# A third Strassen step for one raw product of blocks, and PSUM cut into three pairs and two single banks

## The chip, the cores and the metric

The kernel runs on one core of one Trainium2 chip. The metric is device time in microseconds of one execution. TensorE (PE) multiplies, VectorE (DVE) and ScalarE (ACT) read its sums out of PSUM and prepare its operands, SyncE (SP) issues most of the transfers.

## The reference, cut to what matters

Input x has 8 sequences of 256 rows and 1024 columns, all in float32. Layer one adds a dense product, a routed adapter of rank 16 per expert (two of eight experts per row) and x itself; layer two adds a product with one of 16 dense weights, chosen for each sequence:

```python
# layer one
base = jnp.einsum('btd,od->bto', x, W)
logits = jnp.einsum('btd,ed->bte', x, Wr) + bias[:, None, :]
topw, topi = jax.lax.top_k(logits, 2)
weights = jax.nn.softmax(topw, axis=-1)
gates = jnp.sum(jax.nn.one_hot(topi, E) * weights[..., None], axis=-2)
h = jnp.einsum('btd,erd->bter', x, A)
x = x + base + 2.0 * jnp.einsum('bter,bte,eor->bto', h, gates, B)
# layer two
w = weight[adapter_ids]
x = x + jnp.einsum('bsi,boi->bso', x, w)
```

## The kernel before, in words

Nothing is left to a scheduler: the order of the Python calls is the order of each engine's queue (a manual schedule). The tile layer puts semaphores between the engines where tiles are shared.

**Layer one** is W (1024 x 1024) times x (1024 x 2048 tokens). It is cut into 2 x 2 blocks and done with Winograd's form of Strassen's scheme: seven products of blocks, called "1" to "7", in the order 1, 5, 2, 6, 3, 7, 4. Product 1 is `opening` (L398), the other six are calls of `product` (L442). Each product (512 x 512 by 512 x 1024) is again cut into 2 x 2 and done with seven smaller products, each of four 128x512 matmuls: two row groups m by two depths k. The sums of blocks that these need are s1 to s3 (of W's blocks) and t1 to t3 (of x's blocks), made on VectorE by `make_subs` (L336); `late` (L358) turns s2 and t2 into the fourth sums. In `product` the seven stand in this order, by PSUM tile: A = a00 x b00; B = s1 x t1; A += s2 x t2; X = a01 x b10; A += s3 x t3; B += s2 x b11 (s2 is the fourth sum by now); A += a11 x t2. So a00 x b00 and a01 x b10 (X) are the two products of raw blocks. After each, `evict` (L372) adds the PSUM tile into a quarter of the result y on VectorE (L183), or, where there is nothing to add to, copies it on ScalarE (L375).

A PSUM tile is `bank` (L87): 128 partitions x 2 x 512 float32, so two of the eight banks; the pool turns four of them round.

In four of the six (5, 2, 3, 4) two more matmuls per quarter add the adapter's rows, from `hg` (the gated inner values, turned) and `b_sb` or `bdiff` (L379 to 395).

**The adapter** is prepared between product 1 and product 5. `project(j, c)` (L203) multiplies a quarter of the tokens by the adapter and router weights, 32 matmuls of 136 columns into one PSUM tile; VectorE then makes the logits `lg`, and ScalarE copies the rest to `hT`. `gating(j)` (L249) is some twenty small VectorE instructions and one of 1024 columns. `turn(j)` (L282) turns hT with eight TensorE transposes and copies them to `hg` on ScalarE, in one instruction:

```python
def turn(j):
    ps_g = bank(f"ps_g_{j}")
    for n in range(C):
        nc.tensor.transpose(ps_g[:, n // CQ, ts(n % CQ, P)], hT[j][:, n, :], ident)
    nc.scalar.copy(hg[j], ps_g)
```

The calls between the products stand at L644 to L697: project(1, 0), project(1, 1), gating(1), the sums of product 5 on VectorE, project(0, 1), turn(1), product 5, turn(0), product 2.

**What VectorE does besides.** `todo` is a list of VectorE work for later products (sums of blocks of W and x, the sub-sums of the next product, joins of results). `pump(place)` (L305) stands after each of the seven smaller products and puts an even share of what is left into VectorE's queue there; each entry has a cost and a first place at which it may go.

**Layer two** (`adapt`, L531) does the same for each of the eight sequences with one Strassen step. It uses the same four PSUM tiles, but only half of each. The last sequence (`adapt_last`, L589) splits three of its products into 256-column halves (tile A_last).

Of the kernel before, what the change touches and what calls it, by code (L numbers as in the profile page):

```python
# [9 lines left out]
F32 = mybir.dt.float32  # L10
# [15 lines left out]
def kernel(  # L26
# [48 lines left out]
    sub2 = ctx.enter_context(tc.tile_pool(name="sub2", bufs=2))  # L75
    rpool = ctx.enter_context(tc.tile_pool(name="rpool", bufs=1))
    psum = ctx.enter_context(tc.tile_pool(name="psum", bufs=4, space=PSUM))

# [5 lines left out]
    def flat(blk):  # L84
        return blk.rearrange("p k n -> p (k n)")

    def bank(name):  # L87
        return psum.tile([P, 2, TQ], F32, name=name, tag="acc")

# [9 lines left out]
    aw_sb = flat(yb["12"])[:, : KC * EA].rearrange("p (k e) -> p k e", k=KC)  # L99
    hT = [flat(yb["11"])[:, j * C * ER : (j + 1) * C * ER].rearrange("p (c e) -> p c e", c=C) for j in range(2)]  # L100
    b_sb = const.tile([ER, O], F32, name="b_sb")
    ids = const.tile([1, 2, NB], I32, name="ids")
# [82 lines left out]
    def add(out_, x, y):  # L185
        tt(out_, x, y, ALU.add)

    def minus(out_, x, y):
        tt(out_, x, y, ALU.subtract)
# [7 lines left out]
    hg = [const.tile([ER, 2, TQ], F32, name=f"hg{j}") for j in range(2)]  # L197
    lg = [rpool.tile([P, C, E], F32, name=f"lg_{j}", tag=f"lg{j}") for j in range(2)]
    gate8 = {}

    projected = {}

    def project(j, c, *some, first=True, last=True):  # L203


        if first:
            projected[j, c] = bank(f"ps_h_{j}_{c}")
        ps = projected[j, c]
        some = some or range(KC)
        for k in some:  # L210
            for r in range(CQ):
                v, u = divmod(r, 2)
                nc.tensor.matmul(  # L213
                    ps[:, v, u * EA : (u + 1) * EA],
                    lhsT=xk(k, j, c)[:, ts(r, P)],
                    rhs=aw_sb[:, k, :],
                    start=(first and k == some[0] and u == 0),
                    stop=(last and k == some[-1]),
                    skip_group_check=True,
                )  # L220
        if not last:
            return
        ps = ps[:, :, : 2 * EA].rearrange("p v (u e) -> p v u e", u=2)
        split = lambda t: t[:, c * CQ : (c + 1) * CQ, :].rearrange("p (v u) e -> p v u e", v=2)
        nb = CQ * P // S
        b0 = (2 * j + c) * nb
        add(
            split(lg[j]),
            ps[:, :, :, ER:],
            bias[:, b0 : b0 + nb, :].unsqueeze(2).to_broadcast([P, nb, CQ // nb, E]),  # L230
        )
        nc.scalar.copy(split(hT[j]), ps[:, :, :, :ER])

    def first_max(src, j, n):

        m = rpool.tile([P, C], F32, name=f"m{n}_{j}", tag=f"m{n}")
        place = rpool.tile([P, C, E], F32, name=f"place{n}_{j}", tag=f"place{n}")
        first = rpool.tile([P, C], F32, name=f"first{n}_{j}", tag=f"first{n}")
        hot = rpool.tile([P, C, E], F32, name=f"hot{n}_{j}", tag=f"hot{n}")
        wide = [P, C, E]  # L240
# [8 lines left out]
    def gating(j):  # L249

        m1, hot1, ops1 = first_max(lg[j], j, 1)
        rest = rpool.tile([P, C, E], F32, name=f"rest_{j}", tag="rest")
        m2, hot2, ops2 = first_max(rest, j, 2)
        dm = rpool.tile([P, C], F32, name=f"dm_{j}", tag="dm")
        ex = rpool.tile([P, C], F32, name=f"ex_{j}", tag="ex")
        den = rpool.tile([P, C], F32, name=f"den_{j}", tag="den")
        g1 = rpool.tile([P, C], F32, name=f"g1_{j}", tag="g1")
        g2 = rpool.tile([P, C], F32, name=f"g2_{j}", tag="g2")
        wide = [P, C, E]
# [21 lines left out]

    def turn(j):  # L282

        ps_g = bank(f"ps_g_{j}")
        for n in range(C):
            nc.tensor.transpose(ps_g[:, n // CQ, ts(n % CQ, P)], hT[j][:, n, :], ident)  # L286
        nc.scalar.copy(hg[j], ps_g)

# [46 lines left out]

    def make_subs(key, w, x):  # L336

# [5 lines left out]
        def b(i, j):  # L343
            return xb[x][:, 2 * i : 2 * i + 2, j * TQ : (j + 1) * TQ]

        t = {}

        def op(name, fn, x, y, first):
# [8 lines left out]

        def late():  # L358
            minus(t["s2"], a(0, 1), t["s2"])
            minus(t["t2"], b(1, 0), t["t2"])  # L360

        subs[key] = (a, b, t, late)
        return [
            op("s1", add, a(1, 0), a(1, 1), 2),
            op("t1", minus, b(0, 1), b(0, 0), 2),
            op("s2", minus, "s1", a(0, 0), 2),
            op("t2", minus, b(1, 1), "t1", 2),
            op("s3", minus, a(0, 0), a(1, 0), 5),
            op("t3", minus, b(1, 1), b(0, 1), 5),
        ]  # L370

# [7 lines left out]
    def multiply(up=None, tokens=None):  # L379


        def mm(acc, lhs, rhs, first=False, rows=None, c=0, part=(0, 1)):
            steps = [(lhs[:, k, ts(m, P)], rhs[:, k, :], m) for k in part for m in range(2)]
            if up is not None and rows is not None:
                steps += [(up[rows][:, ts(m, P)], hg[tokens][:, c, :], m) for m in range(2)]
            for i, (l, r, m) in enumerate(steps):
                nc.tensor.matmul(  # L387
                    acc[:, m, :],
                    lhsT=l,
                    rhs=r,  # L390
                    start=(first and i < 2),
                    stop=(i >= len(steps) - 2),
                    skip_group_check=True,
                )

        return mm

    def opening(key, dest):  # L398


        idle = bank("idle")
        for i in range(WARM):
            nc.tensor.matmul(idle[:, 0, :P], lhsT=ident, rhs=ident, start=True, stop=True)  # L403
        mm = multiply()
        sums_of = make_subs(key, "11", "11")
        a, b, t, late = subs.pop(key)
        X = bank(f"X_{key}")
        A = bank(f"A_{key}")
        add_identity(wb["11"], 0, 2)
        mm(X, a(0, 1), b(1, 0), True, part=(0,))  # L410
        project(0, 0, 2, last=False)
        mm(X, a(0, 1), b(1, 0), part=(1,))
        evict(dest[:, 0], X)
        project(0, 0, 3, first=False, last=False)
        mm(A, a(0, 0), b(0, 0), True, part=(0,))
        project(0, 0, 0, first=False, last=False)
        mm(A, a(0, 0), b(0, 0), part=(1,))
        project(0, 0, 1, first=False, last=False)
        use_adapter_ids()
# [5 lines left out]
        use_ids(idle[:, 1, :NB])  # L425
        B = bank(f"B_{key}")
        mm(B, t["s1"], t["t1"], True)
# [4 lines left out]
        evict(dest[:, 1], A)  # L432
        project(0, 0, *range(KH, KC), first=False)
        late()
        mm(A, t["s3"], t["t3"])
# [6 lines left out]
    def product(key, base, dest, lora=None, tokens=None):  # L442

        a, b, t, late = subs.pop(key)
        mm = multiply(dict(zip("01d", b_part(lora))) if lora is not None else None, tokens)
        old = [base[:, q] if base is not None else None for q in range(4)]
        A = bank(f"A_{key}")
        mm(A, a(0, 0), b(0, 0), True)
        evict(dest[:, 0], A, old[0])
        pump(1)  # L450
        B = bank(f"B_{key}")
        mm(B, t["s1"], t["t1"], True, "1", 1)
        evict(dest[:, 3], B, old[3])
        pump(2)
        mm(A, t["s2"], t["t2"])
        evict(dest[:, 1], A, old[1])
        pump(3)
        X = bank(f"X_{key}")
        mm(X, a(0, 1), b(1, 0), True, "0", 0)
        add(dest[:, 0], X, dest[:, 0])  # L460
        late()
        pump(4)
# [68 lines left out]
    def adapt(u):  # L531
# [3 lines left out]
        w = rawset[u % 2]  # L535
        accs = {}

        def mm(name, lhs, rhs, first=False):
            if first:
                accs[name] = bank(f"{name}1_{u}")[:, 0, :]  # L540
            for k in range(KH):
# [47 lines left out]
    def adapt_last(half, sy, w, z, mm, store):  # L589
# [3 lines left out]
        m = OG // 2  # L593
        accs = [bank(f"A{v}_last")[:, 0, :m] for v in range(2)]
        c11, c12, c21, c22 = (z[i][:, ts(j, OG)] for i in range(2) for j in range(2))
# [53 lines left out]
    subs5[2][2]()  # L649
    project(1, 0)  # L650

# [3 lines left out]
    for k in range(KH):  # L655
        t1(0, k)
    project(1, 1)
    for t in gating(1):
# [4 lines left out]
    for k in range(2, KH):  # L663
        t1(1, k)
    subs5[3][2]()
    subs5[4][2]()
    subs5[5][2]()
    project(0, 1)
    turn(1)
    todo += gating(0)  # L670
    todo += w_sum(minus, "11", "21", "11")
    todo += make_subs("2", "12", "21")
    product("5", None, y22, 1, 1)
    turn(0)
    todo += x_sum(minus, "12", "22", "12")
# [10 lines left out]
    todo += make_subs("7", "21", "11")  # L686
    todo += x_sum(minus, "21", "21", "12")
    todo += join(y12, y21)
    product("3", y22, y12, 2, 1)
    load_w1(0, "12", "22", "11")  # L690
    todo += make_subs("4", "22", "21")
    todo += join(y22, y21)
# [62 lines left out]
```

## Time and profile before

| | us |
|---|---|
| median of 3 runs | 430.58 (430.48 to 431.51) |
| the profiled execution | 431.35 |
| its span | 429.6 |
| PE busy | 424.7 (1222 records; a float32 matmul is two) |
| DVE busy | 272.3 (331 instructions) |
| ACT busy | 32.6 (51 instructions) |
| layer one ends (chain) | 233.75 |

The chain of waits follows the work that ended last back from the end. An instruction on it moves the end when it gets longer. The timeline gives each instruction's start and length in microseconds from the start of the span, and in brackets how long its engine had been idle and who ended that.

### The profile page before, as it was taken

The page shows a single profiled execution, that of the slowest core. Times are in us where ns is not written, and L with a number is a line of the kernel's source. Part 1 is how long each engine was busy: PE and PEld are TensorE (multiplying, and loading weights), DVE is VectorE, ACT ScalarE, POOL GpSimd, SP SyncE. Part 2 cuts the span into 40 slices and gives each one's busy share as a digit, 9 for nine tenths or more (in the row PEclk, how much of TensorE's full clock was granted, in tenths as well). Part 3 has the DMA queues.
Part 4 walks back from the last instruction along what each step waited for, and adds up shares of the span by engine and source line. Part 5 has one row for each costly group of instructions (what it writes and reads, how often), then busy time and mean ns, then how long its engine had stood idle before and what let it go on. Part 6 is the DMA issues. An engine that isn't in the chain of part 4 may idle for free.

```text
span 429.6 us, 3225 instructions
## 1 busy us (share of the span) xinstructions
PE 424.7 (99%) x1222; PEld 212.7 (50%) x1222; DVE 272.3 (63%) x331; ACT 32.6 (8%) x51; POOL 2.0 (0%) x10
## 2 busy tenths in 40 slices
PE   8999999999999999999999999999999999999996
PEld 5566984444444444444444444444444444444574
DVE  2627395658877979779575676665756576665531
ACT  1110104010000000000000101010110101010110
POOL 1000000000000000000000000000000000000000
PEclk9999999999999999999999999999999999999999
DMA  8994000000000140630202276556748375550202
GB/s 287 381 400 206 2 2 0 0 0 0 2 0 0 35 160 2 243 148 0 98 2 98 98 256 224 206 201 204 278 140 309 140 268 220 195 198 0 98 0 98
DMA packets 14303, 55.81 MB, mean 130 GB/s; under 512 B 1232, under 2 KB 3536, under 8 KB 9808
## 3 DMA queue, kind: packets, MB, share of 16 engines
q1 hardware_dynamic: 12976, 54.68, 35.3%
q10 hardware_dynamic: 1248, 0.93, 0.7%
q8 instruction: 9, 0.15, 0.2%
q14 instruction: 6, 0.05, 0.0%
q0 software_dynamic: 64, 0.00, 0.0%
HBM read 47.22 MB, written 8.39 MB: 129 GB/s over the span
## 4 chain that ended last, share of the span: by engine, by line
PE 99%; POOL 0%; ACT 0%; issue 0%; POOLq 0%
PE A L387 24%; PE A L542 22%; PE B L387 14%; PE B L542 13%; PE X L387 8%; PE ps_h L213 7%; PE X L542 6%; PE A_last L600 3%; PE idle L403 1%; PE ps_g L286 0%; ACT z L630 0%; PE idle L424 0%; POOL ident masks.py:199 0%; POOL desc_i L149 0%; POOL ident masks.py:197 0%
## 5 line engine op out<-in xcount | busy, mean ns | idle before, releaser
L542 PE MATMUL B<-x,x 128*128 128x512 f32 x128 | 57.5, 592 | 0.0
L387 PE MATMUL A<-t,s 128*128 128x512 f32 x112 | 50.3, 592 | 0.0
L183 DVE TENSOR_TENSOR y<-A,y 128x1024 f32<-128x1024 f32 x23 | 28.1, 1223 | 20.1 <-PE A L387 20.1
L542 PE MATMUL A<-w,x 128*128 128x512 f32 x88 | 39.6, 592 | 0.0
L542 PE MATMUL A<-w,y 128*128 128x512 f32 x88 | 39.1, 592 | 0.0
L542 PEld LDWEIGHTS B<-x,x 128*128 128x128 f32 x128 | 24.3, 190 | 29.8 <-issue 29.7
L183 DVE TENSOR_TENSOR w<-w,w 128x1024 f32<-128x1024 f32 x24 | 29.0, 1222 | 15.4 <-PE A L542 15.3
L387 PEld LDWEIGHTS A<-t,s 128*128 128x128 f32 x112 | 21.2, 190 | 26.3 <-issue 26.3
L375 ACT COPY z<-A 128x512 f32<-128x512 f32 x21 | 12.3, 586 | 272.0 <-PE A L542 272.0
L213 PEld LDWEIGHTS ps_h<-y,x 128*128 128x128 f32 x256 | 30.7, 191 | 3.4 <-issue 3.4
L213 PE MATMUL ps_h<-y,x 128*128 128x136 f32 x256 | 30.6, 279 | 0.0
L542 PEld LDWEIGHTS A<-w,x 128*128 128x128 f32 x88 | 16.7, 190 | 21.0 <-issue 21.0
L542 PEld LDWEIGHTS A<-w,y 128*128 128x128 f32 x88 | 16.7, 190 | 21.0 <-issue 21.0
L387 PE MATMUL X<-x,w 128*128 128x512 f32 x56 | 27.1, 627 | 0.0
L387 PE MATMUL A<-x,w 128*128 128x512 f32 x56 | 25.3, 592 | 0.0
L387 PE MATMUL B<-t,s 128*128 128x512 f32 x56 | 25.3, 594 | 0.0
L387 PE MATMUL B<-x,s 128*128 128x512 f32 x56 | 25.2, 592 | 0.0
L387 PE MATMUL A<-t,w 128*128 128x512 f32 x56 | 25.2, 592 | 0.0
L183 DVE TENSOR_TENSOR y<-B,y 128x1024 f32<-128x1024 f32 x12 | 14.7, 1224 | 15.7 <-PE B L387 15.7
L183 DVE TENSOR_TENSOR x<-x,x 128x1024 f32<-128x1024 f32 (+1 forms) x20 | 19.3, 1004 | 0.0
L387 PEld LDWEIGHTS X<-x,w 128*128 128x128 f32 x56 | 11.0, 200 | 13.1 <-issue 12.8
L387 PEld LDWEIGHTS A<-t,w 128*128 128x128 f32 x56 | 10.6, 190 | 13.4 <-issue 13.4
(109 smaller groups left out, 398.3 us busy)
## 6 DMA issues: line engine op xcount, KB each, us to landing
x<-w_dram SPq DMA_DIRECT2D x24, 1024.0 KB, 4.8
w<-w_dram SPq DMA_DIRECT2D x8, 1024.0 KB, 4.7
out_dram<-z SPq DMA_DIRECT2D x15, 512.0 KB, 3.1
x<-xT_dram SPq DMA_DIRECT2D x6, 1024.0 KB, 13.6
w<-wT_dram SPq DMA_DIRECT2D x3, 1024.0 KB, 15.6
x<-xT_dram SPq DMA_DIRECT2D x4, 256.0 KB, 3.8
x<-xT_dram SPq DMA_DIRECT2D x2, 512.0 KB, 6.7
w<-w11T_dram SPq DMA_DIRECT2D x1, 512.0 KB, 5.4
```

The costliest lines, as they stand in the source:

```text
L183: nc.vector.tensor_tensor(out_, x, y, op)
L213: nc.tensor.matmul(ps[:, v, u * EA : (u + 1) * EA], lhsT=xk(k, j, c)[:, ts(r, P)], rhs=aw_sb[:, k, :], start=(first and k == some[0] and u ...
L375: nc.scalar.copy(dest, acc)
L387: nc.tensor.matmul(acc[:, m, :], lhsT=l, rhs=r, start=(first and i < 2), stop=(i >= len(steps) - 2), skip_group_check=True,)
L403: nc.tensor.matmul(idle[:, 0, :P], lhsT=ident, rhs=ident, start=True, stop=True)
L542: nc.tensor.matmul(accs[name], lhsT=lhs[:, k // 2, k % 2, :], rhs=rhs[:, k, :], start=(first and k == 0), stop=(k == KH - 1), skip_group_c ...
L600: nc.tensor.matmul(acc, lhsT=lhs[:, k // 2, k % 2, :], rhs=rhs[:, k, ts(v, m)], start=(first and k == 0), stop=(k == KH - 1), skip_group_c ...
```

## The change

Three things.

1. **X is computed by a third step.** In `product`, X = a01 x b10 (four 128x512 matmuls) becomes Winograd's seven products of 128 x 128 by 128 x 256. VectorE makes six sums per product for it beforehand (r1, r2, r4 with 128 columns, q1, q2, q4 with 256), and two more (r3, q3) inside it. ScalarE copies A (a00 x b00) into X's pair, and three of the seven are added onto that copy. The first product goes to a single bank, A3, the second and third of the scheme to B3 and A3 again. The first quarter of the result is put together from A3 (quarter by quarter), B3 and X on VectorE. B's matmuls are split: row group 0 before A's second product, row group 1 after it. `late` is split into its two sums, moved ahead of X.
2. **PSUM is laid out by name**: three pairs of banks (`pair0` to `pair2`) and two single banks. A, X and B change pairs from product to product (`roles`). The projections and turns take pairs or singles; their readers work half by half.
3. **The small tiles of the gating** move into a free part of y12, to make room for the deep sums; four sums of x21 are put into `todo` in two halves ("P5" in the list of the change is the split of B's product).

```diff
+    def pair(name, n):
+        return psum.tile([P, 2, TQ], F32, name=name, tag=f"pair{n}")
+    def single(name, n):
+        return psum.tile([P, TQ], F32, name=name, tag=f"single{n}")
+    def halves(pair_):
+        return [pair_[:, v, :] for v in range(2)]
+    def singles(name):
+        return [single(f"{name}{v}", v) for v in range(2)]
+    role = [2, 1, 0]
+    def roles(name):
+        a, x, b = role
+        role[:] = [x, b, a]
+        return lambda which: pair(f"{which}_{name}", dict(A=a, X=x, B=b)[which])
...
-        add(
-            split(lg[j]),
-            ps[:, :, :, ER:],
-            bias[:, b0 : b0 + nb, :].unsqueeze(2).to_broadcast([P, nb, CQ // nb, E]),
-        )
-        nc.scalar.copy(split(hT[j]), ps[:, :, :, :ER])
+        b0 = (2 * j + c) * (CQ // 2)
+        for v in range(2):
+            two = slice(c * CQ + 2 * v, c * CQ + 2 * v + 2)
+            h = ps[v][:, : 2 * EA].rearrange("p (u e) -> p u e", u=2)
+            add(lg[j][:, two, :], h[:, :, ER:], bias[:, b0 + v, :].unsqueeze(1).to_broadcast([P, 2, E]))
+            nc.scalar.copy(hT[j][:, two, :], h[:, :, :ER])
...
-    def turn(j):
-        ps_g = bank(f"ps_g_{j}")
-        for n in range(C):
-            nc.tensor.transpose(ps_g[:, n // CQ, ts(n % CQ, P)], hT[j][:, n, :], ident)
-        nc.scalar.copy(hg[j], ps_g)
+    def turn(j, banks):
+        for c, ps_g in enumerate(banks):
+            for n in range(CQ):
+                nc.tensor.transpose(ps_g[:, ts(n, P)], hT[j][:, c * CQ + n, :], ident)
+            nc.scalar.copy(hg[j][:, c, :], ps_g)
...
+        deep = [
+            op3("r1", "r13", add, ra(1, 0), ra(1, 1)),
+            op3("q1", "q13", minus, rb(0, 1), rb(0, 0)),
+            op3("r2", "r2", minus, "r1", ra(0, 0)),
+            op3("q2", "q2", minus, rb(1, 1), "q1"),
+            op3("r4", "r4", minus, ra(0, 1), "r2"),
+            op3("q4", "q4", minus, rb(1, 0), "q2"),
+        ]
...
-            op("s1", add, a(1, 0), a(1, 1), 2),
-            op("t1", minus, b(0, 1), b(0, 0), 2),
-            op("s2", minus, "s1", a(0, 0), 2),
-            op("t2", minus, b(1, 1), "t1", 2),
+            op("s1", add, a(1, 0), a(1, 1), 3),
+            op("t1", minus, b(0, 1), b(0, 0), 3),
+            op("s2", minus, "s1", a(0, 0), 3),
+            op("t2", minus, b(1, 1), "t1", 3),
...
-        idle = bank("idle")
+        idle = pair("idle", 2)
...
-        X = bank(f"X_{key}")
-        A = bank(f"A_{key}")
+        X = pair(f"X_{key}", 0)
+        A = pair(f"A_{key}", 1)
...
-        B = bank(f"B_{key}")
+        B = pair(f"B_{key}", 2)
...
-        A = bank(f"A_{key}")
+        A = new("A")
         mm(A, a(0, 0), b(0, 0), True)
-        evict(dest[:, 0], A, old[0])
+        X = new("X")
+        nc.scalar.copy(X, A)
+        A3 = single(f"A3_{key}", 0)[:, n0]
+        deep(A3, ra(0, 0), rb(0, 0), True)
+        q, o = quarter(0, n0)
+        evict(q, A3, o)
         pump(1)
-        B = bank(f"B_{key}")
-        mm(B, t["s1"], t["t1"], True, "1", 1)
-        evict(dest[:, 3], B, old[3])
-        pump(2)
+        B = new("B")
+        mm(B, t["s1"], t["t1"], True, "1", 1, ms=(0,))
+        B3 = single(f"B3_{key}", 1)[:, n0]
+        deep(B3, t["r1"], t["q1"], True)
+        deep3()
         mm(A, t["s2"], t["t2"])
         evict(dest[:, 1], A, old[1])
+        deep(A3, t["r2"], t["q2"])
+        q, o = quarter(0, n1)
+        evict(q, A3, o)
+        late[0]()
+        pump(2)
+        mm(B, t["s1"], t["t1"], True, "1", 1, ms=(1,))
+        evict(dest[:, 3], B, old[3])
+        late[1]()
         pump(3)
-        X = bank(f"X_{key}")
-        mm(X, a(0, 1), b(1, 0), True, "0", 0)
+        deep(X[:, 0, n0], ra(0, 1), rb(1, 0))
+        deep(X[:, 0, n1], t["r4"], rb(1, 1))
+        deep(X[:, 1, n0], ra(1, 1), t["q4"])
+        mm(X, None, None, False, "0", 0, part=())
+        deep(A3, t["r3"], t["q3"])
+        two = [P, 2, TQ // 2]
+        d1 = dest[:, 0][:, 1, :].rearrange("p (j n) -> p j n", j=2)
+        both = A3.unsqueeze(1).to_broadcast(two)
+        evict(d1, both, old[0][:, 1, :].rearrange("p (j n) -> p j n", j=2) if base is not None else None)
+        add(dest[:, 0][:, :, n1], B3.unsqueeze(1).to_broadcast(two), dest[:, 0][:, :, n1])
         add(dest[:, 0], X, dest[:, 0])
-        late()
         pump(4)
...
-    project(1, 0)
+    project(1, 0, halves(pair("ps_h_1_0", 0)))
...
-    project(1, 1)
+    project(1, 1, halves(pair("ps_h_1_1", 2)))
...
-    subs5[3][2]()
-    subs5[4][2]()
-    subs5[5][2]()
-    project(0, 1)
-    turn(1)
+    for i in range(3, len(subs5)):
+        subs5[i][2]()
+    project(0, 1, singles("ps_h_0_1"))
+    turn(1, halves(pair("ps_g_1", 0)))
...
-    turn(0)
+    turn(0, singles("ps_g_0"))
```

## The prediction

> **What bounds the kernel now.** I read the page first: engine times, then the chain of work that ended last.
>
> ```profile
> span 429.6 us, 3225 instructions
> PE 424.7 (99%) x1222; PEld 212.7 (50%) x1222; DVE 272.3 (63%) x331; ACT 32.6 (8%) x51; POOL 2.0 (0%) x10
> ...
> PE 99%; POOL 0%; ACT 0%; issue 0%; POOLq 0%
> ```
>
> TensorE is never late: 99% of the chain is matmul after matmul, so each column that goes saves its time at once, and each wait on TensorE costs its whole length. VectorE's 63% is a mean over stages; what matters is when its results are due. The chain in order of time gives the prices and the place where I see most trouble:
>
> ```profile
> 1.41 2.93 PE idle L403 x12
> 4.34 3.52 PE X L387 x4
> ...
> 8.78 1.72 PE X L387 x4
> ...
> 16.71 0.31 PE idle L424 x2
> 17.03 3.63 PE B L387 x8
> ...
> 60.34 0.87 PE ps_g L286 x8
> 61.21 3.43 PE A L387 x8
> ...
> 398.55 3.43 PE A L542 x8
> 401.99 3.45 PE A_last L600 x16
> ```
>
> A product of four 128x512 matmuls is eight records (two to a matmul) and 3.43 us, 0.858 each. A_last makes the same columns as eight 128x256 matmuls in 3.45, 0.431 each: half width is half price.
>
> **What TensorE saves.** In six products X's four matmuls (3.43) become seven of half width, 7 x 0.431 = 3.02. That is -0.41 each, **-2.5 us** in six. Everything else that TensorE does keeps its columns (the adapter rows that go into X too).
>
> **What the others get.** Per product VectorE gains six deep sums, three of 128 and three of 256 columns, two more (r3, q3), two 256-column quarters, the 512-column half d1 and the 512-column B3, and mostly loses the 1024-column first eviction (ScalarE copies A to X instead). Prices: in the timeline a next VectorE instruction starts 1.14 after one of 1024 columns and 0.60 to 0.61 after one of 512; this is columns/960 + 0.075, so 0.34 for 256 and 0.21 for 128 (estimates from those rows; the 256-column sums last 0.42). The result is there 0.08 later, and an instruction that needs its predecessor's result starts 0.12 late. So +1.65 + 0.55 + 0.68 + 0.61 + 0.73 - 1.14 = +3.1 per product. It costs nothing where VectorE idles. I laid the built order of the changed kernel end to end with these prices, and looked for matmuls whose wait ends after TensorE is free.
>
> **1. Opening, +0.3.** B now takes the pair in which the adapter numbers were spread ("idle"), so it waits for VectorE's reading of it. The trace has that reading at 17.06, 0.23 long; B starts at 17.03. B would start at 17.33.
>
> **2. turn(1), +8.4.** This is the large one. Before, eight transposes fill ps_g and one ScalarE copy follows; TensorE goes on with A at once, and needs hg only later. In the changed kernel the halves of one pair are turned and copied in turn, and the built order has this:
>
> ```
> 67 L315 Matmult ps_g_414<-ident,y_77 128x128 [waits DVE_49,PE_49,Activation_49]
> 68 L315 Matmult ps_g_414<-ident,y_77 128x128 x3
> 69 L315 Matmult ps_g_414<-ident,y_77 128x128 [waits Activation_49]
> ```
>
> Row 69, the fifth transpose, waits for the 14th count of ScalarE, and the 14th is the copy of the first half of the same pair (the pair is one tile, and its second half waits for the reader of its first). That copy stands in ScalarE's queue behind the two copies of project(0, 1), which wait for VectorE's lg sums, which stand in VectorE's queue behind all sums of product 5. Before:
>
> ```profile
> 64.38 1.22 DVE L183 TENSOR_TENSOR t<-x 128x1024 f32<-128x1024 f32 x1
> 65.52 0.18 DVE L183 TENSOR_TENSOR lg<-ps_h,bias 128x32 f32<-128x32 f32 x1
> ```
> ```profile
> 65.73 0.59 ACT L232 COPY y<-ps_h 128x512 f32<-128x512 f32 x1 [9.44 <-DVE lg L183]
> 66.21 1.02 ACT L287 COPY hg<-ps_g 128x1024 f32<-128x1024 f32 x1
> 67.12 1.03 ACT L375 COPY y<-A 128x1024 f32<-128x1024 f32 x1
> ```
>
> VectorE's lg at 65.52 is 5 us after the transposes, and harmless, because no matmul waits for it. In the changed kernel it comes later: +0.3 (opening), +0.6 (project(1, 1)'s sum is now two, the second after ScalarE's copy of the first half: lg 0.19, copy of 256 columns 0.37, handing over), +1.65 (the six deep sums ahead of it). That is 68.07; +0.21 to the first copy (65.73 - 65.52), two copies of 256 columns at 0.27 (1024 and 512 columns start the next after 0.91 and 0.48), then the copy of 512 lasts 0.59, and 0.04 to hand over: TensorE goes on at 69.45. It stands from 60.34 + 0.30 + four transposes of 0.11 = 61.08. **8.4 us**. Behind the waiting transpose all of product 5 is queued. Bounds: the wait is there or not (0), and the six deep sums by their full 0.42 and 0.29 make it 8.9.
>
> **3. Product 6, +3.5.** Its last group A (a11 x t2) adds to a pair whose earlier sum VectorE must have read before (into dest 3, "y<-A"). In the kernel before that reading began 1.2 us after its matmuls, because VectorE was busy:
>
> ```profile
> 137.66 1.23 DVE L183 TENSOR_TENSOR y<-X,y 128x1024 f32<-128x1024 f32 x1 [1.07 <-PE X L387]
> 138.80 0.68 DVE L183 TENSOR_TENSOR s<-w,s 128x512 f32<-128x512 f32 x1
> 139.40 1.22 DVE L183 TENSOR_TENSOR t<-x,t 128x1024 f32<-128x1024 f32 x1
> 140.53 0.69 DVE L183 TENSOR_TENSOR s<-s,w 128x512 f32<-128x512 f32 x1
> 141.14 1.22 DVE L183 TENSOR_TENSOR t<-x,t 128x1024 f32<-128x1024 f32 x1
> 142.27 1.22 DVE L183 TENSOR_TENSOR y<-A,y 128x1024 f32<-128x1024 f32 x1
> ```
>
> It ended at 143.49, a microsecond before A at 144.49: that is the slack. Now B's eviction and both late sums fall into this stretch as well. From A's s2 x t2 on, VectorE has nine instructions of 1024 columns (A, two x sums, B, late t, t1, X, t2, A: 8 x 1.14 + 1.22), five of 512 (late s, s1, d1, B3, s2: 3.05), one of 256 (0.34) and two waits for its own result (0.24): 13.97. TensorE in that time has A3, half of B, three of X, A3, A and B: 0.43 + 1.72 + 1.29 + 0.43 + 3.43 + 3.43 = 10.73. With 0.23 of handing over (A's reader starts 0.19 after the next group's first matmul, 134.22 against 134.03; 0.04 back) TensorE stands 3.5.
>
> **4. Product 7, +2.3; product 2, +0.3.** The same sum. Product 7: six full instructions, five of 512, four deep sums and a quarter 1.44, own waits 0.24, the last A 1.22: 12.79 + 0.23 against 10.73. Product 2: ten of 1024 (11.48), 3.05, 0.34, 0.24 = 15.11 + 0.23, against 10.73 and five adapter-row matmuls (15.02). Products 3 and 4 have 15.02 and less on VectorE: no wait. Product 5 evicts on ScalarE: none. Each of these could be 0.5 off either way.
>
> **5. The clock, +2.6.** The trace of before has no gap on TensorE, so this is bounded. After its first idleness TensorE ran at half rate: the first four X records took 3.52, later ones 1.72 (1.80 lost), and the twelve records before, 2.93 where half of A_last's 0.216 makes 1.29 (1.64 more): 3.4 lost. If the 8.4 us stand brings the clock down, the restart loses between 1.8 and 3.4, otherwise 0. I take 2.6, the middle of the two rows, because the stand is longer than the whole slow start (1.41 to 7.86).
>
> The Trainium skill ("TensorE: Matmul & The Clock Gate", Part 1: The HAM clock gate) says that the clock halves after an idle window of about 3.4 us and comes back after a busy one. By that rule, as an estimate, the restart loses 1.7 to 3.4, and the sum would be 444.6 to 446.3; it also says that the 3.5 us stand in product 6 is on the edge. No row of before shows a restart in mid-kernel.
>
> **ScalarE and the rest, 0.** The copy of A to X (0.91) is due only after A3, half of B and B3, 2.58 later. Layer two's code and DMAs are unchanged and only start later; SP's loads wait for the same tiles.
>
> **Sum.** -2.5 + 0.3 + 8.4 + 3.5 + 2.3 + 0.3 + 2.6 = +14.9. The profiled execution took 431.35 (span 429.6 and 1.75 around it), 0.77 over the median of the runs, 430.58. So 446.3 for such an execution, and **445.5** against the median.
>
> **Rivals.**
> - *All sums hidden, faster:* VectorE idles 157 us, and if its queue is never late at a matmul, -2.5 stands: 428.1. For it: 63%. Against: it must finish U's reading before TensorE's return, with 1.0 us of slack in product 6 and 3.1 added; from about 1.0 added it decides, and the fifth transpose must not wait either. 3%.
> - *The transposes don't wait as I read it, the three products do:* -2.5 + 0.3 + 6.1 = 434.5. For it: the halves lie in different banks; against: the wait in the built order. 5%.
> - *The clock stays up:* 442.9. 18%.
> - *The clock falls a second time*, in product 6's 3.5 us: 1.8 to 3.4 more, 448. 10%.
> - *It doesn't do what it says* (half width not at half price): A_last's row excludes it.
> - My forecast: 64%.
>
> **Numbers.** Range 442.3 to 448.5: from the clock staying up with 0.6 less waiting to the second fall; outside lie the two cheap rivals and some of the errors. A measurement here tells 0.3% (1.3 us) from no change. Faster 3%, same 1%, slower 96%.
>
> **What would show it.** TensorE idle about 8.4 us near 61 to 69.5, ended by ScalarE's hg copy; X L387's successor with 256 columns at 0.43 each; matmuls of product 5 at 0.86 a record for some microseconds after the gap; VectorE without a gap from about 143 to 157, and TensorE waiting for "y<-A" in products 6 and 7. If TensorE shows no gap at the transposes, step 2 is wrong; if the three later gaps are missing, my VectorE prices or the slack are.

## The result and the profile after

The changed kernel takes 448.62 us in the median (448.0 to 448.92), the kernel before 430.86 beside it: a ratio of 1.0409, interval 1.039 to 1.0427. The forecast was 445.5, in a range of 442.3 to 448.5; the median lies 0.1 above its upper end. But the forecast started from 430.58 for the kernel before. As a difference the result is +17.8, against +14.9 in a range of +11.7 to +17.9: just inside. The profiled execution took 448.48, 17.1 us more than that of before.

The page of the changed kernel first: its engine times, and its chain by engine.

```profile
span 446.7 us, 3380 instructions
PE 427.5 (96%) x1258; PEld 221.2 (50%) x1258; DVE 290.0 (65%) x399; ACT 39.6 (9%) x65; POOL 2.0 (0%) x10
...
PEclk9999987999999989999899999999999999999999
...
PE 82%; DVE 13%; DMA 2%; issue 1%; ACT 0%; ACTq 0%; DVEq 0%
```

Before, the chain was 99% TensorE. Now VectorE holds 13% of it, and TensorE's granted clock, which before was full in all slices, dips in three places. PE's busy time hardly tells: slow matmuls count as busy.

The chain in order of time at the first dip shows how step 2 looks from the chain: VectorE's sums without a pause (t, s, t, then r and q; the last 4.6 us of them are shown), two ScalarE copies, hg, and only then the last four transposes; product 5's A then takes 5.37 in place of 3.43.

```profile
62.07 1.22 DVE t L217
63.29 0.60 DVE s L217
63.90 1.14 DVE t L217
...
66.31 0.33 DVE q L217
66.76 0.65 ACT y L261 x2
67.41 0.50 ACT hg L316
67.95 1.11 PE ps_g L315 x4
69.07 5.37 PE A L446 x8
```

TensorE's own timeline at the three gaps has in brackets how long it stood, and who let it go. The third line is product 2's group behind its short wait, for comparison:

```profile
59.01 0.60 PE L315 MATMUL ps_g<-ident,y 128*128 128x128 f32 x4
67.95 1.11 PE L315 MATMUL ps_g<-ident,y 128*128 128x128 f32 x4 [8.34 <-ACT hg L316]
...
127.86 3.70 PE L446 MATMUL A<-t,w 128*128 128x512 f32 x8
...
156.76 5.40 PE L446 MATMUL A<-t,w 128*128 128x512 f32 x8 [3.30 <-DVE y L217]
...
214.96 5.40 PE L446 MATMUL A<-t,w 128*128 128x512 f32 x8 [2.12 <-DVE y L217]
```

(The bracket counts from the modelled end of the matmul before, so it is 0.16 less than the time lost from start to start: the gaps cost 8.5, 3.5 and 2.3. Product 2's wait, 0.3 from start to start, is too short for a bracket.) A group of eight records takes 3.60 in this view when it follows another, and 3.70 behind a wait, as in product 2, where the clock was up. Behind the gaps of products 6 and 7 it takes 5.40, so 1.7 more. The view by stretches has the granted clock in its third column from the right, around product 6's gap (153.5 to 156.8):

```profile
156.00:158.00 2.00, 1.24 (x3) 0.68 (x4) 2.00 (x3) 0.00 (x0) 0.00 (x0) 1.00 0.00 0
158.00:160.00 2.00, 2.00 (x4) 0.81 (x3) 2.00 (x4) 0.00 (x0) 0.00 (x0) 0.54 0.00 0
160.00:162.00 2.00, 2.00 (x5) 0.73 (x3) 0.32 (x2) 0.00 (x0) 0.00 (x0) 0.61 0.00 0
162.00:164.00 2.00, 2.00 (x6) 0.95 (x5) 1.80 (x4) 0.00 (x0) 0.00 (x0) 1.00 0.41 61
```

Here the clock falls 1.4 us after TensorE is back at work, and the slow stretch is some 3.4 us long; at half rate that is the 1.7. At turn(1) it was otherwise: the clock fell at about 62.6, while TensorE still stood, and came back at about 72.8, some 10.2 us later (0.54 granted over 62 to 70, 0.50 over 70 to 72, 0.79 over 72 to 74). TensorE was at work in the last 4.9 of them, which cost 2.4.

Stage by stage, from the two chains (start of one stage to the start of the next):

| stage | before | after | difference | of it |
|---|---|---|---|---|
| to project(1, 0) | 38.10 | 36.93 | -1.17 | the clock came up earlier |
| projections, turn(1) | 23.11 | 32.14 | +9.03 | wait 8.5, four transposes at half rate 0.45 |
| product 5 | 30.90 | 32.42 | +1.52 | -0.41, half rate 1.93 |
| product 2 (with turn(0) ahead) | 31.78 | 31.79 | +0.01 | -0.41, wait 0.3, the group behind it 0.1 longer |
| product 6 | 24.03 | 28.89 | +4.86 | -0.41, wait 3.5, half rate 1.7, the group behind the wait 0.1 |
| product 3 | 30.90 | 30.49 | -0.41 | |
| product 7 | 24.03 | 27.71 | +3.68 | -0.41, wait 2.3, half rate 1.7, the group behind the wait 0.1 |
| product 4 | 30.90 | 30.49 | -0.41 | |
| layer two | 192.37 | 192.38 | 0.0 | |

What VectorE did while TensorE stood in product 6 is in the chain, from 142.83 to 156.7 without a pause. Its start and its end:

```profile
142.83 1.55 DVE y L217 x2
...
154.44 1.14 DVE t L217
155.58 1.15 DVE y L217
156.76 8.83 PE A L446 x16
```

The last y is the reading of A's earlier sum that the matmuls of the last group wait for.

### The profile page after: what moved, and what is told of

The parts are those of the page before. It is cut to its first block, busy times and chain, and to the rows that moved or that the text cites. A ratio compares the mean times of both kernels' runs of the same rounds, so it can differ in the third digit from the quotient of the medians.

```text
span 446.7 us, 3380 instructions
## 1 busy us (share of the span) xinstructions
PE 427.5 (96%) x1258; PEld 221.2 (50%) x1258; DVE 290.0 (65%) x399; ACT 39.6 (9%) x65; POOL 2.0 (0%) x10
## 4 chain that ended last, share of the span: by engine, by line
PE 82%; DVE 13%; DMA 2%; issue 1%; ACT 0%; ACTq 0%; DVEq 0%
PE A L634 22%; PE A L446 21%; PE B L634 12%; PE B L446 10%; PE X L634 6%; DVE y L217 5%; PE ps_h L246 4%; DVE t L217 3%; PE A_last L692 3%; DVE x L217 2%; DMA x<-xT_dram 1%; DVE s L217 1%; PE A L511 1%; PE X L446 1%; PE X L511 1%
## 5 line engine op out<-in xcount | busy, mean ns | idle before, releaser
L217 DVE TENSOR_TENSOR y<-A,y 128x1024 f32<-128x1024 f32 (+2 forms) x33 | 29.2, 898 | 28.5 <-PE A L446 15.1
L446 PE MATMUL A<-t,w 128*128 128x512 f32 x56 | 28.9, 665 | 5.6 <-DVE y L217 5.4
L446 PE MATMUL A<-x,w 128*128 128x512 f32 x56 | 27.3, 631 | 0.0
L446 PE MATMUL B<-t,s 128*128 128x512 f32 x56 | 26.3, 594 | 0.3 <-DVE bias L200 0.3
L434 ACT COPY z<-A 128x512 f32<-128x512 f32 x21 | 12.3, 585 | 158.3 <-PE A L634 158.3
L217 DVE TENSOR_TENSOR y<-B,y 128x1024 f32<-128x1024 f32 (+1 forms) x18 | 18.8, 1045 | 6.3 <-PE B L446 5.4
L446 PEld LDWEIGHTS A<-t,w 128*128 128x128 f32 x56 | 11.5, 210 | 21.8 <-issue 13.8
L446 PEld LDWEIGHTS A<-x,w 128*128 128x128 f32 x56 | 11.2, 206 | 13.1 <-issue 13.1
L217 DVE TENSOR_TENSOR t<-x 128x1024 f32<-128x1024 f32 x14 | 17.1, 1221 | 0.6 <-DMA x<-xT_dram 0.5
```

Source lines behind the costliest of these rows:

```text
L217: nc.vector.tensor_tensor(out_, x, y, op)
L434: nc.scalar.copy(dest, acc)
L446: nc.tensor.matmul(acc[:, m, :], lhsT=l, rhs=r, start=(first and i < len(ms)), stop=(i >= len(steps) - len(ms)), skip_group_check=True,)
```

## The experiments

My theory after this: TensorE's saving is real (0.41 in each of six products), and three causes stand against it, namely the order of ScalarE's queue behind VectorE's at turn(1), VectorE's work ahead of one reading in products 6 and 7, and the clock that falls behind such a gap. The rivals are with each run.

**The transposes: one copy, as before the change.** (`one_copy`)

```diff
-    turn(1, halves(pair("ps_g_1", 0)))
+    turn(1, pair("ps_g_1", 0))     # eight transposes, then nc.scalar.copy(hg[j], pair)
```

> The changed kernel, but turn(1) fills both halves of its pair and ScalarE copies them in one instruction, as before the change. My theory: the wait at the fifth transpose goes, but part of it comes back at once. The new layout puts project(0, 1) into the two single banks, and product 5's first half-width matmul takes the first of them (A3). It must wait for ScalarE's copy out of that bank, which stands behind the same lg sums of VectorE: from 63.3 (transposes done at 59.9, A 3.43) to about 67.2, 3.9 us, and B's adapter matmul then 0.8 for hg. So 4.6 of waiting instead of 8.3, and the clock still falls once: about 444.5 us. Rival, the split copy is the whole cause: neither gap nor slow clock there, 8.3 + 2.4 less, about 438.

It took 443.99 (442.66 to 447.06). The fifth transpose no longer waits, and A3 of product 5 does. From TensorE's waits:

```profile
PE A L451 <- DVE y L217: 5.4, 2, 3.3
PE A L516 <- ACT y L261: 3.7, 1, 3.7
```

L516 is the deep matmul, L261 the copy out of project(0, 1)'s bank. So the split copy was only the first in a row: the rival (438) falls. The 0.8 expected at B's adapter rows does not show. A second wait on the same ScalarE instructions lay hidden behind the first; the prediction had not named it.

**The transposes: ScalarE's order.** (`readers_behind`)

```diff
-    project(0, 1, singles("ps_h_0_1"))
+    rest01 = project(0, 1, singles("ps_h_0_1"), read=False)   # matmuls only
     turn(1, halves(pair("ps_g_1", 0)))
+    rest01()                                                  # lg sums and hT copies
```

> The changed kernel with turn(1) in halves, but the two lg sums and hT copies of project(0, 1) are issued after turn(1), so that ScalarE copies hg first. Theory: the fifth transpose then waits only for one copy of 512 columns (0.6) and its handing over, 0.8 in all, and A3 of product 5 waits for the hT copy as in the run with one copy, some 3.1 to 3.3: 4 us instead of 8.3, clock still down once, about 444.2 us. Rival, the fifth transpose waits for VectorE's queue itself and not for ScalarE's order: no change, 448.6.

443.95 (438.11 to 444.51). The profiled execution, the one of 438.11, has the two expected waits, 0.7 and 2.8 where 0.8 and 3.1 to 3.3 were expected:

```profile
PE A L517 <- ACT y L267: 2.8, 1, 2.8
...
PE ps_g L321 <- ACT hg L322: 0.7, 1, 0.7
```

So the fifth transpose waited for the order of ScalarE's queue and not for VectorE as such. In that one execution the clock did not fall at all, though the gaps of 3.3 and 2.12 in products 6 and 7 are both there; the other four lie 5.4 to 6.4 higher.

**The layout alone.** (`layout_alone`) the six products are made as before the change and without deep sums, the rest is the changed kernel (the first place of s1, t1, s2 and t2 in `todo` stays 3, as there):

```diff
+    SHALLOW = ("2", "3", "4", "5", "6", "7")   # X = four full matmuls, no deep sums
```

> The new PSUM layout, projections and turns of the changed kernel, but all six products as before the change (X in four full matmuls, first eviction on VectorE, late in one place, no deep sums). Theory: the layout alone costs most of the loss: the fifth transpose waits 8.3 less the deep sums' 1.7, 6.6 us, and the clock falls once (1.9 and 0.45 of slow transposes); products 2, 6 and 7 have no gap. 430.9 + 0.3 + 6.6 + 2.4 = 440.2, or 1.2 less if the clock comes up a window earlier in the opening. Rival, the third step's work is the cause of all waits: 431.

439.89 (439.49 to 440.36), and beside the opening's 0.3 one wait:

```profile
PE ps_g L316 <- ACT hg L317: 6.7, 1, 6.7
```

So some 9 of the 17.8 us (439.89 against 431.15 of before beside it) have nothing to do with the third step: they come with the new layout, the wait of turn(1)'s second half first, and the slow clock behind it. The rival (431) falls. The deep sums lengthen this wait by 8.34 - 6.73 = 1.6, the 1.65 of the prediction.

**Useless matmuls in the gaps.** (`filler`)

```diff
+            if j == 1 and c == 1:
+                filler(pair("filler_1", 1)[:, 0, :], 9)
...
+        if key in FILL:                    # {"6": 3, "7": 2}
+            filler(single(f"filler_{key}", 0), FILL[key])
```

> The changed kernel with matmuls of no use put into TensorE's three gaps: nine of 128x512 ahead of the fifth transpose (7.7 of 8.3 us), three ahead of product 6's last group (2.6 of 3.3), two ahead of product 7's (1.7 of 2.1). The waits end when they ended before. Theory: the half-rate stretches behind the gaps come from the idleness itself, so the granted clock stays at 1.00 and 2.4 + 2.0 + 2.0 are saved: about 442.3 us. Rival, the matmuls behind a gap are slow for another reason (the engine restarting, VectorE or ScalarE at work beside it): 448.6 or more.

443.14 (442.79 to 443.58): 5.5 us are won by giving TensorE more to do. Around turn(1) and product 6 the clock stays full:

```profile
58.00:70.00 12.00, 11.38 (x43) 6.14 (x42) 11.13 (x26) 1.72 (x4) 0.00 (x0) 1.00 0.01 1
70.00:80.00 10.00, 10.00 (x27) 4.95 (x26) 1.29 (x4) 1.95 (x3) 0.00 (x0) 1.00 0.00 0
150.00:165.00 15.00, 14.28 (x36) 6.44 (x35) 13.01 (x18) 1.00 (x1) 0.00 (x0) 1.00 0.34 113
```

The half rate comes from the idleness. And without it the sum of the prediction is met: 430.9 - 2.5 + 0.3 + 8.4 + 0.3 + 3.5 + 2.3 = 443.2. The expected 442.3 was 0.8 too low: it put 2.0 on each of the two later falls, where the timeline has 1.7.

**Every wait of the adapter part taken away.** (`turn_fixed`)

```diff
-        B = pair(f"B_{key}", 2)                      # opening
+        B = pair(f"B_{key}", 0)
...
     subs5[1][2]()                                    # t1 of product 5
+    rest01 = project(0, 1, singles("ps_h_0_1"), read=False)
+    turn(1, pair("ps_g_1", 0))                       # one copy
+    rest01()                                         # ahead of t2, deep sums, s3, t3
```

> The changed kernel with every wait between product 1 and product 5 taken away: one copy for turn(1); the readers of project(0, 1) issued behind turn(1) on ScalarE and, on VectorE, right after t1 of product 5, ahead of its other sums; B of the opening in pair 0, so that it doesn't wait for the reading of the adapter numbers. All six third steps stay. Theory: no gap and no slow clock until product 2; the three VectorE gaps stay (0.2, 3.3, 2.1): 430.9 - 2.5 + 5.6 = 434.0 with the clock up all the time, 1.7 to 1.9 more for each of the two gaps behind which it falls: 434 to 438. Rival, the gaps of products 6 and 7 came from what happened in the adapter part: 428.4.

436.36 (436.15 to 438.29). TensorE's only waits after the start are VectorE's, 5.4 in two, 3.3 the longest, as in the changed kernel. So the gaps of products 6 and 7 stand on their own; the rival (428.4) falls. In the profiled execution the clock fell behind product 6's gap and stayed up behind product 7's, so the two groups of eight show the price of one fall side by side, 1.7:

```profile
146.56 5.39 PE L457 MATMUL A<-t,w 128*128 128x512 f32 x8 [3.31 <-DVE y L217]
...
204.76 3.70 PE L457 MATMUL A<-t,w 128*128 128x512 f32 x8 [2.12 <-DVE y L217]
```

**VectorE's part of the third step left out** (`no_sums`), on top of the run before.

```diff
+        t.update(r1=ra(1, 0), q1=rb(0, 1), r2=ra(1, 1), ...)   # raw blocks
...
-        ] + (deep if further else [])
+        ]
...
-        deep3()
...
-        evict(d1, both, ...)                                   # product 5: nc.scalar.copy
-        add(dest[:, 0][:, :, n1], B3.unsqueeze(1).to_broadcast(two), dest[:, 0][:, :, n1])
...
     product("6", y21, y21)
     load_w1(0, "21")
+    todo += t3[2:]                                             # was ahead of product 6
```

> As the run turn_fixed, with TensorE's third step whole, but VectorE's part of it left out: the half-width matmuls read raw blocks in place of the sums r and q, the B3 and d1 additions are not made (product 5 keeps a copy for d1), and product 6's last two x sums are made in product 3. The result is not the reference's. Theory: TensorE has no gap and the third step is worth what its columns say, 430.9 - 2.5 = 428.4. Rival, matmuls of half width cost more here than in the last sequence, or the copies of A to X and the single banks cost TensorE something: 430 or more.

428.82 (428.56 to 429.18), 0.9958 of before (0.9943 to 0.9974), so 1.8 us less, between 1.1 and 2.5. The list of TensorE's waits has none after the start. The expected 2.5 is at the edge of the interval; in the chain products 5, 2, 6 and 3 are 0.41 shorter each, and 0.3 is lost where product 7 ends and product 4 begins. The third step is worth to TensorE about what its columns say, and the rival (430 or more) falls.

**The same work of VectorE in another order** (`sums_later`), all six third steps, on top of turn_fixed.

```diff
-            op("s2", minus, "s1", a(0, 0), 3),
-            op("t2", minus, b(1, 1), "t1", 3),
+            op("s2", minus, "s1", a(0, 0), 5),
+            op("t2", minus, b(1, 1), "t1", 5),
...
-        def op3(name, tag, fn, x, y, first=4):
+        def op3(name, tag, fn, x, y, first=5):
...
     product("6", y21, y21)
     load_w1(0, "21")
+    todo += t3[2:]
```

> As the run turn_fixed, all six third steps, all of VectorE's work kept, but in another order: s2, t2 and the deep sums of the next product may go into VectorE's queue only from the fifth place of a product (behind the reading of A that TensorE waits for), and product 6's last two x sums go into product 3. Theory: what counts is what stands ahead of that one reading. Product 6's 13.97 us lose two x sums, s2 and t2 (4.0) and product 7's 12.8 lose t2, s2 and four deep sums (2.9); other places get tighter. Laid end to end: gaps of 0.9 in product 2, 0.6 in 6, 0.8 in 7 and 1.3 at product 4's first B, 3.6 in all in place of 5.6, each too short to bring the clock down: 430.6 - 2.5 + 3.6 = 431.7. Rival, VectorE is simply full in products 6 and 7 and the order doesn't matter: 436 as in turn_fixed.

431.91 (431.17 to 432.51), the expected 431.7. Its waits:

```profile
PE A L457 <- DVE y L217: 1.7, 3, 0.7
...
PE B L457 <- DVE y L217: 0.9, 1, 0.9
```

Four short gaps, 2.6 in all, where two long ones were, 5.4, and no fall of the clock in the profiled execution. That accounts for the 4.4 us against turn_fixed: 2.8 of waits and 1.7 for the one fall. Much of the loss in products 6 and 7 was the order ahead of one reading; the rival (436) falls. What VectorE has too much of in these two products moves on with the order and shows at the next places.

**GpSimd takes a share.** (`gpsimd_sums`)

```diff
-            op("s1", add, a(1, 0), a(1, 1), 3),
+            op("s1", g_add, a(1, 0), a(1, 1), 3),    # nc.gpsimd.tensor_tensor; s2, s3, r, q alike
...
-    todo += t3[2:]
+    todo[:0] = [(0.0, 0, f) for f in t3g]            # two x sums on GpSimd
```

> As the run turn_fixed with all six third steps, but GpSimd, idle otherwise, makes the r, q, s1, s2 and s3 sums of products 2, 6, 3, 7 and 4 and two x sums of product 6 (two w sums of product 6 are moved ahead). VectorE loses about 1.2 + 1.65 of work per product and 2.3 more in product 6. If GpSimd needs up to 3 ns per column and leaves VectorE alone: gaps of 0.1 at most, 428.4 us. Rival, VectorE's instructions get longer while GpSimd reads and writes beside them: the gaps of products 6 and 7 come back, 431 to 438.

432.09 (431.39 to 432.36): the rival. From the groups of VectorE, shapes kept apart:

```profile
L218 DVE TENSOR_TENSOR y<-A,y 128x1024 f32<-128x1024 f32 x18 | 21.9, 1219 | 20.4 <-PE A L465 15.2 <-issue 5.2
L218 DVE TENSOR_TENSOR t<-x 128x1024 f32<-128x1024 f32 x14 | 21.8, 1556 | 0.3 <-DMA x<-xT_dram 0.3
L218 DVE TENSOR_TENSOR t<-x,t 128x1024 f32<-128x1024 f32 x14 | 19.7, 1404 | 0.0
```

t sums, two inputs from SBUF, last 1.56 and 1.40 in the mean where they lasted 1.22; y<-A, with one input from PSUM, stays at 1.22. The longest beside GpSimd sums took 3.36. Gaps of 1.6 and 1.3 are left in products 7 and 6. In product 7 two t sums ahead of the awaited reading, of 2.28 and 1.90, are 1.7 longer than plain ones, and in product 6 two, of 2.28 and 1.55, 1.4 longer, so the lengthening accounts for the gaps.

**The third step only where the adapter gives VectorE time.** (`four_deep`) On top of turn_fixed, products 6 and 7 as before the change:

```diff
+    SHALLOW = ("6", "7")
...
-        ] + (deep if further else [])
+        ] + (deep if further and key not in SHALLOW else [])
...
+        if key in SHALLOW:
+            return plain(key, base, dest, lora, tokens)    # the product of before
```

> As the run turn_fixed, but products 6 and 7, which have no adapter matmuls, are made as before the change (X in four full matmuls, no deep sums). Products 5, 2, 3 and 4 keep the third step. Theory: in these four TensorE has five or six adapter matmuls more, VectorE keeps up, and there is no gap: 430.9 - 4 x 0.41 = 429.2, faster than the kernel before by 0.4%. Rival, a gap of 0.2 or more stays in product 2 or 3 and takes back half, or the new layout costs something on its own: 430 to 431.

428.53 (428.36 to 429.18): 0.9952 of before, interval 0.9938 to 0.9965, so 2.1 us less (1.5 to 2.7), where 1.65 was expected. This beats both kernels. In its chain products 5, 2, 3 and 4 take 30.49, 31.36, 30.48 and 30.48, 0.41 less each than before, and products 6 and 7, with the new layout and no third step, 24.03 and 24.04 as before. So 1.65 is the third step. The rest of the difference between the two profiles is in the opening, 0.84, where the clock came up earlier (its first four X records, "4.34 2.68 PE X L458 x4" here, took 3.52 before), and that is not the change's. Its chain over product 5 shows TensorE going from one group to the next without a gap, with the deep matmuls (L559) at their half price:

```profile
59.50 0.87 PE ps_g L322 x8
60.38 3.44 PE A L458 x8
63.81 0.43 PE A L559 x2
64.24 2.58 PE B L458 x6
66.82 0.43 PE B L559 x2
67.25 3.43 PE A L458 x8
70.68 0.43 PE A L559 x2
71.11 2.58 PE B L458 x6
73.69 1.29 PE X L559 x6
```

## Why the prediction came out as it did

- **What TensorE saves, -2.5: right.** Products 3 and 4, which have neither wait nor slow clock, are 0.41 shorter each; a half-width matmul is 0.43.
- **Opening, +0.3: the wait was right** (0.3 for VectorE's "bias" on the page), the stage was not: it got 1.2 shorter. The first four records of X took 2.16 where before they took 3.68, because the clock came up some 3 us earlier. Nothing in the change did that: in the eleven profiles taken the same four records took 2.0 to 3.7, and the profile of before has the longest.
- **turn(1), +8.4: right**, 8.34 (8.5 from start to start), by the chain that was named: VectorE's sums, lg, two copies, hg. What the prediction missed is the second wait behind it (A3 for ScalarE's copy out of its bank, 2.8 to 3.7), which costs nothing as long as the first stands, but takes back half of a repair.
- **Product 6, +3.5, product 7, +2.3, product 2, +0.3: right.** 3.5, 2.3 and 0.3 from start to start. VectorE's stretch in product 6 was laid at 13.97, and runs from 142.83 to 156.71, 13.88.
- **The clock, +2.6: the mis-sized term.** The mechanism was right, and the first fall cost 1.93 + 0.45 = 2.4. But the forecast had the clock fall once, and in the profiled execution it fell three times: 1.7 more behind each of the gaps of 3.3 and 2.12, 5.8 in all. A second fall was a rival with 10%, at 1.8 to 3.4; a third, behind a gap of 2.12, was in no rival. That the result is still inside the range is partly luck: the range's upper end was drawn for two falls, and three cheaper ones fitted under it. "TensorE: Matmul & The Clock Gate", Part 1, of the Trainium skill speaks of an idle window of about 3.4 us; the trace shows slow stretches of that length behind the two later gaps, and these gaps are shorter than it. The measurement decides.
- **The sum.** -2.5 + 0.3 + 8.4 + 0.3 + 3.5 + 2.3 = 12.3 for waits and columns: the run with useless matmuls, 443.14 against 431.15 of before beside it, gives 12.0. The rest of the 17.8, 5.8, is the clock, where 2.6 was set; the profiled execution's three falls come to the same 5.8.
- **The rivals.** All sums hidden (428.1): excluded by the three gaps that end with VectorE's reading. The transposes don't wait (434.5): excluded by the 8.34. The clock stays up: excluded by the three slow stretches; with the gaps filled it is what happens.

## What to carry to other kernels

Where TensorE is 99% of the chain, look not for the mean share of the helping engine but for each reading that a matmul waits for, and add up what stands in the queue ahead of it: product 6 had 1.0 us to spare there, got new sums, and had B's eviction and the late sums moved ahead of that reading; TensorE stood 3.5. Cutting one reader of a PSUM tile into two made the second writer wait here for the first reader, and that reader for all that its engine had queued (8.3 us); put such readers at the head of their queues first. A saving on the bounding engine belongs only where the helper has time: the change as made loses 17.8 us, and the same third step in the four products that have adapter matmuls, with the queues at turn(1) put right, wins 2.1 in the medians, of which the stages give 1.65 to the third step.

## What the runs showed of the hardware

- The granted clock fell for stretches of about 3.4 us, or of two or three times that (10.2 at turn(1) in the changed kernel), which do not follow the matmuls: the same gap of 2.12 in product 7 brought it down in the changed kernel and in the run with one copy, and not in the profiles of readers_behind and turn_fixed; the gap of 3.3 in product 6 brought it down in three of the four profiles that have it. What decides between them no run here shows. One fall behind these gaps cost 1.7 in four cases (a group of eight at 5.4 in place of 3.70) and 2.9 in one (6.60, product 6 in one_copy). Gaps up to 1.6 (gpsimd_sums) brought it down in no profile taken here. This makes the time of a kernel with gaps of 2 to 4 us spread by several microseconds (438.11 to 444.51 in one case) from one execution to the next.
- GpSimd's float32 sums of two SBUF inputs took 3.3 us for 1024 columns and in the mean 1.4 to 2.0 for 512 (gpsimd_sums), against VectorE's 1.22 and 0.68. Beside them some of VectorE's sums of two SBUF inputs lasted longer, up to 3.36 in place of 1.22, and others did not; its sums with a PSUM input kept their 1.22.
- Without GpSimd beside it VectorE's instructions lasted as long as before (1.22 for 1024 columns, 0.68 for 512, 0.42 for 256), whatever else was changed, so a queue laid end to end by hand met the trace within 0.1 in 14 us.
